# An expert's gathered tokens in three tiles instead of two, and the sums of hT inside the branch

## The chip, the core and the metric

The kernel runs on one core of a Trainium2 chip. The metric is the device time of one execution in microseconds (us). Three timed runs of the kernel before gave 5443.06, 5445.47 and 5447.21 us; the median is 5445.47 us. A profiled execution of the same kernel is what the prediction reads.

TensorE multiplies, VectorE and ScalarE work on tiles in on-chip memory, GpSimd issues the indirect transfers (gathers and scatters by index), and SyncE's queue issues nearly all other transfers. The profile calls them PE (with PEld for its weight loads), DVE, ACT, POOL and SP.

## What is computed

One decoder layer in f32: `x` of 8 sequences x 512 tokens x 512 features goes through a Mamba block, a cross-attention with 16 heads, and a mixture of experts, each followed by a residual sum and a layer norm. Only the last part matters here; the reference cut to it:

```
cap = int(1.25 * N * K / E)            # N = 4096 tokens, K = 4, E = 32: cap = 640
w, idx = _gate(xf, wg)                 # 4 experts and 4 weights for each token
...                                    # place of each token in its experts' buffers
xe = xp[buf_tok].reshape(E, cap, DIM)
h = silu(einsum('ecd,edh->ech', xe, w1)) * einsum('ecd,edh->ech', xe, w3)
out = einsum('ech,ehd->ecd', h, w2) * buf_w.reshape(E, cap, 1)
y = zeros((N + 1, DIM)).at[buf_tok].add(out.reshape(E * cap, DIM))[:N]
z = silu(xf @ sw1) * (xf @ sw3) @ sw2  # a shared expert, for all tokens
return (y + z).reshape(shape)
```

All three matrices of an expert are 512 x 512. An expert has room for 640 tokens; how many it gets depends on the data.

## The kernel before

`program` runs three stages: `layers` (Mamba, attention, the gate, the shared expert, and a scatter of every token's row into `xbuf`, ordered by expert), `experts` (32 experts, one after the other), and `finish` (the last layer norm). The diff touches `experts` alone.

**What an expert does.** `load(e)` starts four transfers on SyncE's queue (ScalarE's for the weights of expert 0): the tile `xe` with the expert's 640 gathered rows, five groups j = 0 to 4 of 128 rows, each row with its 32 expert weights and its token number behind it, and the weights w1, w3 and w2. `flip` turns one group's rows by four PE transposes into PSUM (`ps_t`, two buffers), and DVE copies them into `xT`. The matmuls are done by a Strassen scheme: seven products of half-sized blocks instead of eight, at the price of sums on DVE: `sums_w` makes the four sums of w1 and of w3, `sums_x` those of xT, `sums_w2` those of w2, and `sums_w(got, "hT")` those of `hT`, the hidden layer. `hidden` computes hT = silu(x w1) * (x w3) in two halves r; `give` computes hT w2, multiplies by the tokens' weights (`use` on DVE, `keep` on ACT), and `put(j)` adds each group of 128 result rows into `based` by an indirect DMA that GpSimd issues. The adding transfers go one after the other.

**The branch.** `hidden` comes in four copies, for 224, 256, 288 or 320 columns in a half; `tc.Switch` jumps to the copy that the number of the expert's tokens asks for (`arm`, a table written by the gate). A copy also holds the first two flips of the next expert and `fifth`, the product of the last group of rows (at 288 and 320 columns; otherwise DVE clears that result). PE, ACT and DVE each jump into a copy and, at its end, out of it to the code that all copies share. Each of the three engines announces its next jump ahead of time: `announce` places a load of the table's entry and a prefetch hint behind a given instruction of that engine.

**The order.** All instructions are written in program order, unrolled over the 32 experts. A planner that works with its own cost model may reorder them within a block, but nothing moves across the edge of a copy. In iteration e, `load(e + 1)` comes first, then the branch with `hidden(e)`, the next expert's first two flips and `fifth(e)`, then `give(e)`. Into `give` the helper `between` mixes the next expert's remaining flips, its `sums_w` of w3 and its `sums_x`.

**Buffers.** `xe`, `xT` and the weights have two buffers each (`p2` and `wp` have `bufs=2`), `hT` and its sums one. The tile xe of expert e is in use until the last `put` of expert e has landed, since the token numbers in it steer that transfer. So `xe` of expert e + 2 goes into the buffer of expert e, and its transfer waits for that landing.

In the profile the lines are: `xe` transfer L1258, weight transfers L1261, transposes L1294, their copies L1296, sums of w1, w3 and hT L1288, sums of xT L1303 to L1306, sums of w2 L1321, all products L1328 (`ps_h` in `hidden`, `ps_o` in `give`), ACT's copies L1343 and L1415, DVE's work in `hidden` L1350 and L1354, DVE's clearing of unused columns at the head of a copy L1521, `fifth` L1398, DVE's additions in `use` L1421, and `put` L1424.

Of the kernel before, what the change touches and what calls it, by code (L numbers as in the profile page):

```python
# [8 lines left out]
F32 = mybir.dt.float32  # L9
# [3 lines left out]
ALU = mybir.AluOpType  # L13
# [4 lines left out]
P = 128  # L18
# [21 lines left out]
E = 32  # L40
# [7 lines left out]
CJ = CAP // P  # L48
# [3 lines left out]
ROW = D + E + 1  # L52
# [1175 lines left out]
def experts(ctx, tc, a, xbuf, based, arm):  # L1228
# [11 lines left out]
    nc = tc.nc  # L1240
    cp = ctx.enter_context(tc.tile_pool(name="e_const", bufs=1))
    wp = ctx.enter_context(tc.tile_pool(name="e_w", bufs=2))
    p2 = ctx.enter_context(tc.tile_pool(name="e_p2", bufs=2))
# [7 lines left out]
    FH = D // 2  # L1251

    def load(e):
        got = {}
        got["x"] = xe = p2.tile([P, CJ, ROW], F32, tag="xe", name="xe")

        start = nc.sync.dma_start if e else nc.scalar.dma_start
        nc.sync.dma_start(xe, xbuf[e * CAP : (e + 1) * CAP, :].rearrange("(j p) d -> p j d", p=P))  # L1258
        for n in ("w1", "w3", "w2"):
            got[n] = w = wp.tile([P, DC, D], F32, tag=n, name=n)  # L1260
            start(w, a[n][e].rearrange("(c p) f -> p c f", p=P))  # L1261
        return got

    def A(w, i, j):
        return w[:, 2 * j : 2 * j + 2, i * FH : (i + 1) * FH]

    def BW(w, j, k):
        return w[:, 2 * j : 2 * j + 2, k * FH : (k + 1) * FH]
# [4 lines left out]
    def room_w(got, n):  # L1273

        s1, s2, s4 = (wp.tile([P, 2, FH], F32, tag=f"{n}s{i}", name="s", bufs=1 if n == "hT" else 2) for i in (1, 2, 4))
        got[n, "s"] = s1, s2, A(got[n], 1, 0), s4

    def sums_w(got, n):

        w = got[n]  # L1280
        s1, s2, _, s4 = got[n, "s"]
        for o, x, y, op in (
            (s1, A(w, 1, 0), A(w, 1, 1), ALU.add),
            (s2, s1, A(w, 0, 0), ALU.subtract),
            (A(w, 1, 0), A(w, 0, 0), A(w, 1, 0), ALU.subtract),
            (s4, A(w, 0, 1), s2, ALU.subtract),
        ):
            yield nc.vector.tensor_tensor(o, x, y, op)  # L1288

    def flip(got, j):  # L1290

        ps = pst.tile([P, D], F32, tag="tr", name="ps_t")
        for dc in range(DC):
            nc.tensor.transpose(ps[:, dc * P : (dc + 1) * P], got["x"][:, j, dc * P : (dc + 1) * P], ident)  # L1294
        to = got["xT"].rearrange("p c (k t) -> p c k t", k=2)[:, :, :, j * P // 2 : (j + 1) * P // 2]
        nc.vector.tensor_copy(to, ps.rearrange("p (c t k) -> p c k t", c=DC, k=2))  # L1296
# [11 lines left out]
    def room_w2(got):  # L1308
        got["t2"] = [wp.tile([P, 2, FH], F32, tag=f"w2t{i}", name="t", bufs=1) for i in range(4)]

    def sums_w2(got):

        w = got["w2"]
        t1, t2, t3, t4 = got["t2"]
        for o, x, y in (
            (t1, BW(w, 0, 1), BW(w, 0, 0)),
            (t2, BW(w, 1, 1), t1),
            (t3, BW(w, 1, 1), BW(w, 0, 1)),
            (t4, BW(w, 1, 0), t2),
        ):  # L1320
            nc.vector.tensor_tensor(o, x, y, ALU.subtract)  # L1321
            yield

    def product(ps, w, r, x, more=False):

        cols = ps.shape[-1]
        for n in range(2):
            ins = nc.tensor.matmul(  # L1328
                ps, w[:, n, r * P : (r + 1) * P], x[:, n, 0:cols], start=not more and n == 0, stop=n == 1,
                skip_group_check=more,  # L1330
            )
        return ins
# [57 lines left out]
    def fifth(e, got, cols):  # L1390

        j, y = CJ - 1, got["y"][CJ - 1]
        if 2 * cols <= j * P:
            nc.vector.memset(y, 0.0)
            return
        po = pso.tile([P, D], F32, tag="po", name="po")
        for ic in range(DC):
            nc.tensor.matmul(  # L1398
                po, got["hT"][:, ic, j * P : (j + 1) * P], got["w2"][:, ic, :], start=(ic == 0), stop=(ic == DC - 1)
            )  # L1400
        nc.scalar.activation(y, po, AF.Identity, scale=got["x"][:, j, D + e : D + e + 1])

    def give(e, got, side, which):

        xe, hT, w2 = got["x"], got["hT"], got["w2"]
        t1, t2, t3, t4 = got["t2"]
        both = range(2)
        ys = got["y"]

        def weight(j):  # L1410
            return xe[:, j, D + e : D + e + 1]

        def keep(ps, r, tag, j):
            v = p2.tile([P, HALF], F32, tag=f"{tag}{r}", name=tag)[:, 0:FH]
            ins = nc.scalar.activation(v, ps, AF.Identity, scale=weight(j))  # L1415
            if tag == "p1" and r and e + 1 < E:
                announce(which, e + 1, ins)
            return v

        def use(j, k, ps, more):  # L1420
            nc.vector.scalar_tensor_tensor(ys[j][:, k * FH : (k + 1) * FH], ps, weight(j), more, ALU.mult, ALU.add)  # L1421

        def put(j):
            nc.gpsimd.indirect_dma_start(  # L1424
                out=based,
                out_offset=bass.IndirectOffsetOnAxis(ap=xe.bitcast(I32)[:, j, D + E :], axis=0),
                in_=ys[j],
                in_offset=None,
                bounds_check=N + P - 1,
                compute_op=ALU.add,  # L1430
            )

        room_w(got, "hT")
        for ins in sums_w(got, "hT"):
            pass
        if e + 1 < E:
            announce(which, e + 1, ins)
        s1, s2, s3, s4 = got["hT", "s"]
        next(side, None)
        xs, p1, pu, p5 = [], [], [], []  # L1440
        for r in both:
            xs.append(psx.tile([P, HALF], F32, tag="h", name="ps_o")[:, 0:FH])
            product(xs[r], A(hT, 0, 0), r, BW(w2, 0, 0))
            p1.append(keep(xs[r], r, "p1", r))

        put(CJ - 1)
        next(side, None)
        for r in both:
            ps = psy.tile([P, HALF], F32, tag="h2", name="ps_o")[:, 0:FH]
            ins = product(ps, A(hT, 0, 1), r, BW(w2, 1, 0))  # L1450
            use(r, 0, ps, p1[r])
        if e + 1 < E:
            announce(which, e + 1, ins)
        for r in both:
            product(xs[r], s2, r, t2, more=True)
            pu.append(keep(xs[r], r, "pu", r))
        next(side, None)
        zs = []
        for r in both:
            zs.append(psy.tile([P, HALF], F32, tag="h2", name="ps_o")[:, 0:FH])  # L1460
            product(zs[r], s1, r, t1)
            p5.append(keep(zs[r], r, "p5", 2 + r))
        for r in both:
            product(xs[r], s3, r, t3, more=True)
            use(2 + r, 1, xs[r], p5[r])
        next(side, None)
        for r in both:
            product(zs[r], s4, r, BW(w2, 1, 1), more=True)
            use(r, 1, zs[r], pu[r])
            put(r)  # L1470
        next(side, None)
        for r in both:
            product(xs[r], A(hT, 1, 1), r, t4, more=True)
            nc.scalar.activation(ys[2 + r][:, 0:FH], xs[r], AF.Identity, scale=weight(2 + r))
            put(2 + r)
# [16 lines left out]
    def choice(k, e):  # L1492
        return engines[k].value_load(arm[0:1, e : e + 1])

    def announce(which, e, ins):
        k = ins.ins.engine
        with tc.issue_after(ins.ins):
            which[k] = choice(k, e)
            tc.switch_hint({k: which[k]}, len(COLS), label=f"cols{e}")
# [10 lines left out]
    which = {k: choice(k, 0) for k in engines}  # L1510
    for e in range(E):
        got, nxt = nxt, load(e + 1) if e + 1 < E else None
        got["hT"] = p2.tile([P, DC, CAP], F32, tag="hT", name="hT", bufs=1)
        room_w2(got)
        got["y"] = [p2.tile([P, D], F32, tag="y", name="y", bufs=CJ + 2) for j in range(CJ)]
        if nxt:
            nxt["xT"] = p2.tile([P, DC, CAP], F32, tag="xT", name="xT")
            room_w(nxt, "w1")
        for n in tc.Switch(which, len(COLS), hint=f"cols{e}" if e else None):
            if COLS[n] < HALF:  # L1520
                nc.vector.memset(got["hT"][:, :, 2 * COLS[n] :], 0.0)  # L1521
            for r in range(2):
                side = sums_w2(got) if r == 0 else sums_w(nxt, "w1") if nxt else iter(())
                hidden(got, r, side, COLS[n])
            if nxt:
                for j in range(2):
                    flip(nxt, j)
            fifth(e, got, COLS[n])
        give(e, got, between(nxt) if nxt else iter(()), which)
# [95 lines left out]
```

## Time and profile before

| what | value |
|---|---|
| median of three runs | 5445.47 us (5443.06 to 5447.21) |
| the profiled execution's own time | 5449.73 us |
| its span, first to last instruction | 5448.0 us |
| granted clock of PE, mean | 0.925 |
| PE busy | 4531.9 us, 83% |
| DVE busy | 4204.0 us, 77% |
| ACT busy | 2549.7 us, 47% |
| first expert's first product, by the timeline | 3800.5 us |
| last expert's first product | 5338.1 us |
| copies taken by the 32 experts | 12 at 224 columns, 5 at 256, 6 at 288, 9 at 320 |

The span is from the first instruction to the last; the execution's own time has 1.7 us around it. Busy shares are means over stages: up to about 3780 us the `layers` stage runs, in which DVE is busiest; the expert stage takes the 1580 us after it, about 49 us for each expert. A line of the waits names the engine, the tile it writes and its line, then what it waited for, the sum of those waits, how many there were, and the longest. A row of the timeline has the start, the duration, the engine, the line, output <- input, shapes, a count, and in brackets the idle time before it with what ended it. "issue" is idle time in which the engine waited for nothing that the profile shows. The columns of the windows are the busy time of each engine, the granted clock of PE and the DMA engines' busy share. The count of copies is from the shapes of the products in `hidden`.

### The profile page before, as it was taken

The numbers are of one execution on the slowest core, as the hardware profiler recorded it, in microseconds if no ns is written. First come the engines' busy times: TensorE is split into PE (matmuls) and PEld (weight loads), VectorE is DVE, ScalarE is ACT, GpSimd is POOL, SyncE is SP. The second block draws the span as 40 slices with busy tenths as digits, with TensorE's granted clock in tenths as the row PEclk, the third lists the DMA queues.
The fourth block names the chain that finished last, engine by engine and source line by source line (L and its number), as shares of the span: only waits on it lengthen the run. The fifth ranks groups of instructions, "written<-read, shape, count | busy, mean of one in ns | idle before, by whom it ended". The sixth has DMA issues, their size and how long they took to land.

```text
span 5448.0 us, 55096 instructions
## 1 busy us (share of the span) xinstructions
PE 4531.9 (83%) x17184; PEld 2469.3 (45%) x17184; DVE 4204.0 (77%) x5412; ACT 2549.7 (47%) x5709; POOL 569.6 (10%) x426
## 2 busy tenths in 40 slices
PE   6768889888888888978888888788978789898984
PEld 3324334234333433423433343233777667767773
DVE  7999899989989889998898988833555555555554
ACT  5566565665655556556565565422222222222223
POOL 1000002002002000200200200001111111111111
PEclk7879989999999998999999999898999999999997
DMA  8875337355435534635543553342454444444445
GB/s 240 266 217 144 93 92 212 75 124 170 119 100 152 151 96 98 204 77 133 165 117 99 154 146 94 85 135 82 106 131 104 128 120 126 109 128 120 114 119 156
DMA packets 486691, 721.80 MB, mean 132 GB/s; under 512 B 117137, under 2 KB 200625, under 8 KB 484096
## 3 DMA queue, kind: packets, MB, share of 16 engines
q1 hardware_dynamic: 450128, 627.16, 40.5%
q0 software_dynamic: 33280, 76.90, 7.3%
q10 hardware_dynamic: 2736, 11.54, 0.5%
q8 instruction: 211, 3.46, 0.3%
q14 instruction: 336, 2.75, 0.1%
HBM read 391.24 MB, written 165.05 MB: 102 GB/s over the span
## 4 chain that ended last, share of the span: by engine, by line
DVE 37%; PE 23%; DMA 16%; issue 16%; ACT 6%; SPq 2%; DVEq 0%; POOL 0%; POOLq 0%; ACTq 0%
DVE h L502 14%; DMA based<-y,xe 9%; PE ps_h L1328 6%; DVE h L495 5%; DVE h L511 5%; PE ps_p L758 3%; PE po L553 3%; DVE mx L823 2%; DVE xs L378 2%; PE ps_s L821 2%; ACT l_da L481 2%; PE ps_t L847 2%; PE po L863 2%; PE ps_o L1328 1%; PE py L522 1%
## 5 line engine op out<-in xcount | busy, mean ns | idle before, releaser
L481 ACT ACTIVATE l_da<-rep,l_aneg 128x256 f32<-128x256 f32 x2048 | 893.7, 499 | 942.8 <-DVE h L502 877.7
L502 DVE TENSOR_TENSOR_SCAN h<-l_da,h 128x1028 f32<-128x1028 f32 x512 | 1163.6, 2286 | 20.9 <-ACT l_da L481 18.4
L495 DVE TENSOR_TENSOR h<-rep,bc 128x1024 f32<-128x1024 f32 x512 | 612.6, 1213 | 108.4 <-PE py L522 90.6
L511 DVE TENSOR_TENSOR h<-h,bc 128x1024 f32<-128x1024 f32 x512 | 617.1, 1212 | 2.1
L522 PE MATMUL py<-h,l_fold 128*32 128x512 f32 x2048 | 369.5, 647 | 110.9 <-DVE h L511 94.2
L821 PE MATMUL ps_s<-l_ka,l_qa 64*128 64x512 f32 x1024 | 328.8, 714 | 140.8 <-DVE mx L823 140.3
L1424 POOL DMA_INDIRECT based<-y,xe x160 | 254.6, 1591 | 1355.9 <-DVE y L1421 530.0
L1328 PE MATMUL ps_h<-xT,w 128*128 128x224 f32 (+3 forms) x1536 | 375.2, 395 | 14.2 <-issue 10.4
L823 DVE TENSOR_REDUCE mx<-ps_s 128x2 f32<-128x1024 f32 x256 | 309.6, 1214 | 61.2 <-PE ps_s L821 60.7
L863 PE MATMUL po<-eT,l_va 128*64 128x512 f32 x1024 | 303.1, 673 | 47.1 <-ACT eT L851 42.1
L1328 PEld LDWEIGHTS ps_h<-xT,w 128*128 128x128 f32 x1536 | 296.3, 193 | 71.9 <-issue 13.1
L847 PE MATMUL ps_t<-l_qa,l_ka 64*128 64x512 f32 x1024 | 304.6, 666 | 24.1 <-ACT eT L851 23.3
L851 ACT ACTIVATE eT<-ps_t 128x1024 f32<-128x1024 f32 x256 | 258.8, 1015 | 128.2 <-PE ps_t L847 128.1
L696 POOL DMA_INDIRECT xbuf<-x2t,dest x128 | 217.2, 1697 | 863.8 <-DVE dest L680 764.2
L1328 PE MATMUL ps_h<-t,s 128*128 128x224 f32 (+3 forms) x1024 | 253.1, 396 | 34.5 <-DVE hT L1350 21.0
L344 PE MATMUL ps_z<-xnT,wm 128*128 128x256 f32 x1024 | 238.8, 390 | 29.6 <-DVE o L562 24.2
L553 PE MATMUL po<-wm,zs 128*128 128x512 f32 x512 | 246.6, 637 | 13.4 <-DVE z L965 11.7
L758 PE MATMUL ps_p<-x2T,wa 128*128 128x512 f32 x512 | 242.3, 628 | 18.0 <-ACT hT L952 10.4
L1350 DVE TENSOR_TENSOR hT<-ps_h,p 128x224 f32<-128x224 f32 (+3 forms) x128 | 55.8, 436 | 260.5 <-PE ps_h L1328 259.5
L344 PE MATMUL ps_x<-xnT,wm 128*128 128x256 f32 x1024 | 247.6, 394 | 4.5 <-ACT xnT L333 2.5
L344 PEld LDWEIGHTS ps_z<-xnT,wm 128*128 128x128 f32 x1024 | 195.6, 194 | 92.0 <-DVE o L562 37.4
L344 PEld LDWEIGHTS ps_x<-xnT,wm 128*128 128x128 f32 x1024 | 196.9, 196 | 82.2 <-issue 45.1
(237 smaller groups left out, 7011.1 us busy)
## 6 DMA issues: line engine op xcount, KB each, us to landing
w<-in_w SPq DMA_DIRECT2D x93, 1024.0 KB
wm<-in_in_proj_w SPq DMA_DIRECT2D x128, 512.0 KB
rep<-dt SPq DMA_DIRECT2D x256, 256.0 KB
rep<-dtx SPq DMA_DIRECT2D x256, 256.0 KB
xbuf<-zero SPq DMA_DIRECT2D x32, 1362.5 KB
xe<-xbuf SPq DMA_DIRECT2D x32, 1362.5 KB
wm<-in_out_proj_w SPq DMA_DIRECT2D x64, 512.0 KB
wa<-in_sw SPq DMA_DIRECT2D x24, 1024.0 KB
```

Source lines behind the costliest of these rows:

```text
L344: nc.tensor.matmul(ps[:, i, :], w[:, dc, i * P : (i + 1) * P], f["xnT"][:, dc, :], start=(dc == 0), stop=(dc == DC - 1),)
L481: nc.scalar.activation(da[:, n, 1:], dt[:, j, i, :], AF.Exp, scale=aneg[:, 2 * q + i, 2 * jj + j, g : g + 1])
L495: nc.vector.tensor_tensor(h[:, :, 1:], dtx.rearrange("p j i t -> p (j i) t"), f["bc", g][0], ALU.mult)
L502: nc.vector.tensor_tensor_scan(flat, da.rearrange("p n t -> p (n t)"), flat, 0.0, ALU.mult, ALU.add)
L511: nc.vector.tensor_tensor(h[:, :, 0:T], h[:, :, 1:], f["bc", g][1], ALU.mult)
L522: nc.tensor.matmul(f["py"][j * QP : (j + 1) * QP, :, :], fold, hs[j // 2][:, 2 * (j % 2) : 2 * (j % 2) + 2, 0:T], start=False, stop=g == N ...
L553: nc.tensor.matmul(pos[j], yg[:, c, j * P : (j + 1) * P], w[:, i, :], start=(c == 0), stop=(c == CC - 1))
L821: nc.tensor.matmul(ps[:, j, :], qa[r, lt * P : (lt + 1) * P], ka[r, :], start=True, stop=True)
L823: return lambda: nc.vector.tensor_reduce(mx[:, lt, :].unsqueeze(2), ps, AX.X, ALU.max) and None
L847: nc.tensor.matmul(ps[:, j, :], ka[r, kc * P : (kc + 1) * P], qa[r, :], start=True, stop=True)
L863: nc.tensor.matmul(po[j * 2 * HD : (j + 1) * 2 * HD, :], va[:, kc, i, j * HD : (j + 2) * HD], eT[:, j, :], start=(kc == 0), stop=(kc == SC ...
L1328: ins = nc.tensor.matmul(ps, w[:, n, r * P : (r + 1) * P], x[:, n, 0:cols], start=not more and n == 0, stop=n == 1, skip_group_check=more,)
```

## The change

Three things:

- `xe` gets a third buffer. Expert e + 3 now shares a buffer with expert e.
- The four sums of hT on DVE move from the start of `give` into each of the four copies, behind `hidden` and ahead of the two flips. Their tiles are taken before the branch.
- DVE's announcement of the next jump had stood behind the last of those sums. It now stands behind the second of the first two additions (`use(r, 0, ...)`) in `give`, beside PE's announcement. For that `use` returns its instruction.

```
@@ load
-        got["x"] = xe = p2.tile([P, CJ, ROW], F32, tag="xe", name="xe")
+        got["x"] = xe = p2.tile([P, CJ, ROW], F32, tag="xe", name="xe", bufs=3)
@@ give
         def use(j, k, ps, more):
-            nc.vector.scalar_tensor_tensor(ys[j][:, k * FH : (k + 1) * FH], ps, weight(j), more, ALU.mult, ALU.add)
+            return nc.vector.scalar_tensor_tensor(
+                ys[j][:, k * FH : (k + 1) * FH], ps, weight(j), more, ALU.mult, ALU.add
+            )
...
-        room_w(got, "hT")
-        for ins in sums_w(got, "hT"):
-            pass
-        if e + 1 < E:
-            announce(which, e + 1, ins)
         s1, s2, s3, s4 = got["hT", "s"]
...
         for r in both:
             ps = psy.tile([P, HALF], F32, tag="h2", name="ps_o")[:, 0:FH]
             ins = product(ps, A(hT, 0, 1), r, BW(w2, 1, 0))
-            use(r, 0, ps, p1[r])
+            out = use(r, 0, ps, p1[r])
         if e + 1 < E:
             announce(which, e + 1, ins)
+            announce(which, e + 1, out)
@@ the loop over experts
         room_w2(got)
+        room_w(got, "hT")
...
                 hidden(got, r, side, COLS[n])
+            for _ in sums_w(got, "hT"):
+                pass
             if nxt:
                 for j in range(2):
                     flip(nxt, j)
```

More of the change, by code (lines that the diff above doesn't have):

```diff
@@ L1254, in load @@
         got = {}
-        got["x"] = xe = p2.tile([P, CJ, ROW], F32, tag="xe", name="xe")
+        got["x"] = xe = p2.tile([P, CJ, ROW], F32, tag="xe", name="xe", bufs=3)
         start = nc.sync.dma_start if e else nc.scalar.dma_start
@@ L1420, in use @@
         def use(j, k, ps, more):
-            nc.vector.scalar_tensor_tensor(ys[j][:, k * FH : (k + 1) * FH], ps, weight(j), more, ALU.mult, ALU.add)
+            return nc.vector.scalar_tensor_tensor(
+                ys[j][:, k * FH : (k + 1) * FH], ps, weight(j), more, ALU.mult, ALU.add
+            )
         def put(j):
@@ L1431, in put @@
             )
[L1433 to L1437, printed above, removed]
         s1, s2, s3, s4 = got["hT", "s"]
@@ L1450, in give @@
             ins = product(ps, A(hT, 0, 1), r, BW(w2, 1, 0))
-            use(r, 0, ps, p1[r])
+            out = use(r, 0, ps, p1[r])
         if e + 1 < E:
             announce(which, e + 1, ins)
+            announce(which, e + 1, out)
         for r in both:
@@ L1514, in experts @@
         room_w2(got)
+        room_w(got, "hT")
         got["y"] = [p2.tile([P, D], F32, tag="y", name="y", bufs=CJ + 2) for j in range(CJ)]
@@ L1524, in experts @@
                 hidden(got, r, side, COLS[n])
+            for _ in sums_w(got, "hT"):
+                pass
             if nxt:
```

## The prediction

> **What bounds the kernel now.** I read the waits of the expert stage first, then the timeline of single experts. The waits, in total, number and longest:
>
> ```profile
> DVE s L1288 <- issue: 107.5, 23, 6.1
> ...
> PE ps_t L1294 <- DMA xe<-xbuf: 81.9, 16, 10.5
> ...
> PE ps_o L1328 <- DVE s L1288: 27.0, 16, 3.6
> ...
> PE ps_h L1328 <- DVE hT L1350: 21.0, 24, 2.6
> ```
>
> The second line is the one that the third tile aims at: TensorE waits for xe 81.9 us (10.5 of it ahead of the first expert, which no tile can help; 71.4 inside the stage). The first and third belong to the sums of hT. Where xe's wait comes from shows in the chain of waits and on SyncE's queue, in expert 10 (224 columns):
>
> ```profile
> 4315.47 4.77 DMA based<-y,xe
> ```
>
> ```profile
> 4320.43 0.37 SPq L1258 DMA_DIRECT2D xe<-xbuf  x1
> ```
>
> The last put of expert 9 lands at 4320.24; the transfer of expert 11's xe starts at 4320.43, as both share a buffer. TensorE in the same stretch:
>
> ```profile
> 4317.51 1.68 PE L1328 MATMUL ps_h<-t,w 128*128 128x224 f32 x8
> 4328.10 3.05 PE L1294 MATMUL ps_t<-e_ident,xe 128*128 128x128 f32 x12 [8.90 <-DMA xe<-xbuf]
> ...
> 4347.69 1.49 PE L1328 MATMUL ps_h<-xT,w 128*128 128x224 f32 x7
> ```
>
> TensorE ends `hidden` at 4319.2, idles 8.90 us until xe has landed, and starts the next expert at 4347.69. I call the time from the end of `hidden` to the next expert's first product the tail: here 28.5 us. The loop is xe, flips, products, four puts that go one after the other, next xe; it takes 48 to 53 us in nearly every expert, whatever its columns. Only where `hidden` is short (22.05 us at 224 columns against 31 to 34 at 320) does TensorE come to the flips before xe.
>
> Expert 14, also of 224 columns, found its xe landed, and so shows what the stage is like without that wait. TensorE, then VectorE:
>
> ```profile
> 4525.74 0.63 PE L1294 MATMUL ps_t<-e_ident,xe 128*128 128x128 f32 x4 [0.44 <-DVE xT L1296]
> ...
> 4532.94 3.50 PE L1328 MATMUL ps_o<-t,s 128*128 128x256 f32 x8 [2.68 <-DVE s L1288]
> ...
> 4542.63 1.99 PE L1328 MATMUL ps_o<-t,hT 128*128 128x256 f32 x8 [0.42 <-DVE y L1421]
> ```
>
> ```profile
> 4524.90 1.29 DVE L1296 COPY xT<-ps_t 128x512 f32<-128x512 f32 x2
> 4531.38 0.69 DVE L1288 TENSOR_TENSOR s<-hT 128x512 f32<-128x512 f32 x1 [5.19 <-issue]
> ...
> 4533.92 1.28 DVE L1296 COPY xT<-ps_t 128x512 f32<-128x512 f32 x2
> ...
> 4542.10 0.87 DVE L1421 SCALAR_TENSOR_TENSOR y<-ps_o,xe,p 128x256 f32<-128x256 f32 x2
> ```
>
> Tail: 4524.4 to 4544.4, 20.0 us. VectorE copies the two flips, leaves the copy by a jump and idles 5.19 us on "issue", and only then makes the sums of hT, for which TensorE waits 2.68 us. From 4531.38 VectorE works without a gap to its last additions, and TensorE waits 0.42 us for the first two of those: VectorE's line of work sets this tail. At 320 columns (the last copy, left without a jump) no such idle time shows, and the tail is TensorE's, 18.4 to 19.2 us in seven of nine.
>
> **The third tile.** It removes the wait for the landing in all experts: the transfer of expert e+2 then needs the puts of e-1, which land about 21 us into `hidden(e)`, and its flips come over 40 us later. The transfer is moved on SyncE's queue ahead of w1, w3 and w2 of its own expert. If it stands there for the puts (landed 21 to 23 us into an expert), w1 and w3 behind it, which need the end of `hidden(e)` (22 us at the earliest), lose at most about 1 us; by the DMA queue they land 9 us after issue, and VectorE's first sum of w1 comes 23 us after it. No other queue is passed. A tile takes 640/128 x 545 x 4 = 10.9 KB of a partition and no time.
>
> The gain, by tails read off the timeline. Nine experts at 224 columns waited 3.9 to 8.9 us: 26.8, 27.1, 27.7, 23.6, 27.4, 28.5, 26.4, 28.3, 26.9 us, together 242.7. For the new tail I take 20.3: the two experts of that kind without the wait have 20.0 (14) and 20.9 (29), and 256 columns 21.0. 9 x 20.3 = 182.7, a gain of 60.0. Expert 30 loses its 5.85 us. Three experts with 0.9 to 1.4 us of wait (6, 19, 22) go from 22.4, 21.1, 22.5 to 20.3, 19.9, 20.3: 5.5. Sum 71.4.
>
> **The clock.** After xe's waits TensorE runs at half clock for a while. Windows of it (stretch, its length, busy time and count of PE, PEld, DVE, ACT and POOL, then the granted clock, third from the right):
>
> ```profile
> 4321.60:4331.80 10.20, 3.68 (x15) 3.15 (x16) 1.38 (x2) 0.00 (x0) 1.01 (x1) 0.50 0.99 325
> 4533.20:4536.60 3.40, 3.40 (x10) 2.59 (x10) 3.40 (x7) 0.59 (x2) 0.00 (x0) 0.50 0.02 5
> 4132.00:4142.00 10.00, 5.69 (x27) 4.61 (x28) 8.09 (x14) 1.90 (x4) 0.00 (x0) 1.00 0.16 51
> ```
>
> The first row follows the 8.90 us wait; the second follows expert 14's 2.68 us for the sums; ahead of the third's middle TensorE waited 3.44 us and kept full clock. Of six waits of 2.7 to 3.6 us for the sums, two were followed by half clock. The Trainium skill (TensorE: Matmul & The Clock Gate, What's actually happening) says that an idle window of about 3.4 us halves the clock; by it the shorter waits that this change leaves would cost nothing. The rows allow up to 3.4 us at half clock, 1.7 us of work, after a third of them. I count none, since VectorE sets those tails, and keep 17 x 1.7 / 3 = 10 us for the range.
>
> **The sums of hT.** Per expert four instructions (0.69, 0.69, 0.68, 0.68 us, starting 0.6 apart: 2.5 us) move on VectorE ahead of two copies (1.3 us) and of the jump. In expert 14, from the end of `hidden`: sums 0.5 to 3.0, copies 3.0 to 4.3, idle 5.2, next copies at 9.5. Before: copies 0.5 to 1.8, idle 5.2, sums 7.0 to 9.5, next copies at 9.5. The line has the same pieces in another order, so its end stays. What waits for the moved sums now is the pair of copies: the third flip needs a PSUM buffer that the first copy empties, at 3.7 instead of 1.2, so TensorE idles about 2.4 us there in the 17 experts that have no `fifth` to cover it (its products take 3.6 us in the timeline, at 288 and 320). It then reaches its s2 product at about 8.2, finds the sums ready (instead of 2.68 us of waiting) and is held by VectorE's first additions at about 12.0 instead of 12.4. So of the 27.0 us of waits for the sums I credit 3: 0.7 in each of experts 9, 13 and 29, where the first copies had to wait for TensorE, and 1.2 in the last, where nothing follows, as VectorE's next wait takes the rest.
>
> Against that, the idle time of the jump out. It was 4.5 to 6.1 us where the jump fell into the weight transfers that start as `hidden` ends, 3.9 to 4.7 where xe had delayed it past them, and 2.2 and 2.5 for the last two experts, which load nothing. The jump now comes 2.5 us later, deeper into those transfers: I allow 0.3 us, which is in the 20.3, and at 288 columns a tail of 19.9 where four of six have 19.5 to 19.7: a loss of 1. Net: a gain of 2.
>
> **The announcement.** The load and the hint go from behind the sums (8.5 us or more ahead of the jump) to behind the second addition (about 5 us). Queued behind them on VectorE are the last two sums of w3; the load takes 0.3 us of its sequencer, under a 0.68 us sum. Jumps to the 224 copy, the first in order, show 1.1 to 1.4 us of idle time before L1521 in eleven of twelve cases; jumps to the 256 and 288 copies 2.6 to 4.3 us in ten of eleven, though announced. If the later hint made those prompt, TensorE would get back at most the 21.0 us that it waits for L1350, less 0.3 in each 224 expert: 17. If it made the 224 jumps late too, the one such case (into expert 5, TensorE waiting 2.63 instead of 0.29) prices it: 11 x 2.3 = 26 lost. I take nothing: jumps announced 8 to 14 us ahead came equally late, so the lead is not what decides. The Trainium skill (Runtime: NRT & Kernel Launch, Instruction fetch mechanics) speaks against this change: an engine but TensorE holds two fetch blocks, and a taken branch out of them waits for a transfer. By it no hint's place helps VectorE, the jumps stay, and the sum is the same.
>
> **Sum.** 71.4 + 2 = 73 us. From the profiled 5449.7 that gives 5376.4; that execution lay 4.3 us above the median, so I predict 5372.
>
> **Rivals.** *Eaten by VectorE (19%).* With xe gone, VectorE's jump of 5 to 6 us and its sums are late next, everywhere, and the delayed copies cost what I hid: 1.5 us in 23 experts is 35, leaving a gain of 20 to 50, 5395 to 5425. For it: the tail is VectorE's already. Against: expert 14 shows that tail, and I used it. *More than I count (10%).* The hint works and half of the 24 us of waits for the sums that I did not credit go too: 73 + 17 + 12 = 102, 5343. Against: the line of VectorE has no shorter order. *The transfer is not early (3%).* The planner leaves xe behind a wait on SyncE's queue and the time stays within 0.2%. Against: even behind w2 it starts as `give` ends, 22 us ahead of its flips. *Slower (6%).* The third flip's 2.4 us of idling comes out on the path, with the clock halved after each: 2.4 + 3.4 = 5.8 us in the 17 experts up to 256 columns is 99, minus 73: 26 slower, 5471. It decides from 73 / 17 = 4.3 us for each of them. For it: half clock after 2.68 us. Against: six such waits gave it twice.
>
> **How the numbers follow.** The forecast, a gain of 55 to 95, has 62%. 0.2% is 11 us, about what a measurement of this kernel can tell from no change. The range goes down by the hint's 17 and 15 of the waits for the sums (5340) and up by the jumps' 35 (5407); what lies outside is the rivals' far ends. Faster 0.91, same 0.03, slower 0.06.
>
> **What would show it.** Right: no wait for xe but the first 10.5 us, no row of sums behind "issue" (the idle time now stands before a copy, L1296, still about 5 us in 23 experts), TensorE's waits for the sums at zero, new ones of 2 to 3 us before L1294, tails near 20 us in all experts, and a mean clock above 0.925. Wrong: waits for xe that stay; tails of 22 and more; or heads of the 256 to 320 copies without idle time, which would put the hint to work.

## The result and the profile after

The changed kernel takes 5494.43 us (median of four runs, 5482.32 to 5503.45) against 5445.4 us in the same session: a ratio of 1.0084, 95% interval 1.0071 to 1.0096. By the ratio it is slower by about 46 us (49 by the medians), where 73 less was predicted. The profiled execution took 5503.45 us, its span is 5501.7 us, the granted clock 0.917. Of the 53.7 us by which the spans differ, 9.7 lie ahead of the first expert's first product (3810.2 us against 3800.5); in the profiles of the experiments, none of which touches that stage, this point lies anywhere from 3789 to 3807, so I put no cause to it. The expert stage, from the first product to the last, is 44.7 us longer: 1621.9 us against 1577.2. What follows it is 0.7 us shorter.

The waits of the expert stage after, in the form shown of before:

```profile
PE ps_o L1328 <- DVE y L1421: 141.8, 31, 11.2
DVE s L1288 <- DMA w<-in_w: 114.7, 24, 10.3
...
ACT p L1343 <- issue: 78.8, 15, 5.7
...
PE ps_h L1328 <- ACT p L1343: 37.2, 19, 3.1
...
PE ps_t L1294 <- DVE xT L1296: 22.5, 23, 1.6
...
PE ps_t L1294 <- DMA xe<-xbuf: 10.8, 1, 10.8
```

The same rows of the kernel before, where the prediction does not show them:

```profile
PE ps_o L1328 <- DVE y L1421: 28.2, 35, 0.9
...
ACT p L1343 <- issue: 20.2, 4, 5.4
...
PE ps_h L1328 <- ACT p L1343: 13.3, 10, 2.8
...
DVE s L1288 <- DMA w<-in_w: 9.7, 7, 1.8
```

The third tile did what it says: TensorE waits for xe ahead of the first expert and nowhere else (81.9 us before). The sums of hT are no longer waited for (27.0 before), and their row behind "issue" is gone. In their place TensorE waits 141.8 us for VectorE's first additions (28.2 before), and VectorE 114.7 us for a weight (9.7 before). Those two are one thing. Expert 14 again, which the prediction had taken as its model, VectorE first:

```profile
4556.46 0.69 DVE L1296 COPY xT<-ps_t 128x512 f32<-128x512 f32 x1 [4.29 <-PE ps_o L1328]
4562.86 0.69 DVE L1288 TENSOR_TENSOR s<-w 128x512 f32<-128x512 f32 x1 [5.71 <-DMA w<-in_w]
4563.58 0.69 DVE L1288 TENSOR_TENSOR s<-s,w 128x512 f32<-128x512 f32 x1
4564.19 0.68 DVE L1288 TENSOR_TENSOR w<-w 128x512 f32<-128x512 f32 x1
4564.79 0.68 DVE L1296 COPY xT<-ps_t 128x512 f32<-128x512 f32 x1
4565.40 0.68 DVE L1288 TENSOR_TENSOR s<-w,s 128x512 f32<-128x512 f32 x1
4565.99 0.87 DVE L1421 SCALAR_TENSOR_TENSOR y<-ps_o,xe,p 128x256 f32<-128x256 f32 x2
```

then TensorE, SyncE's queue, and the chain of waits:

```profile
4554.51 1.89 PE L1328 MATMUL ps_o<-t,s 128*128 128x256 f32 x8
4557.21 0.66 PE L1294 MATMUL ps_t<-e_ident,xe 128*128 128x128 f32 x4 [0.81 <-DVE xT L1296]
4566.53 3.78 PE L1328 MATMUL ps_o<-t,s 128*128 128x256 f32 x8 [8.67 <-DVE y L1421]
```

```profile
4548.19 0.37 SPq L1258 DMA_DIRECT2D xe<-xbuf  x1
4548.65 26.56 SPq L1261 DMA_DIRECT2D w<-in_w  x3
```

```profile
4549.22 13.61 DMA w<-in_w
...
4562.86 0.70 DVE s L1288
```

TensorE ends `hidden` at 4547.95; xe's transfer starts at 4548.19 and w1's and w3's at once behind it. VectorE idles 4.29 us behind the jump (the profile puts this wait down to a product, but the flip that the copy reads had ended 5.9 us before). It copies the third flip, and then, before the fourth flip and the first additions, stands 5.71 us for w3, until 4562.86. It makes three sums of w3, a copy, the fourth sum, and only then the additions, at 4565.99, 18.1 us after `hidden`. TensorE has idled 8.67 us for them, and its next products run at half clock: eight of one kind take 3.78 us where eight of the same kind took 1.89 before the wait, and the windows (columns as in the prediction) give

```profile
4550.00:4557.50 7.50, 6.65 (x35) 5.36 (x36) 2.86 (x5) 1.89 (x4) 0.58 (x1) 1.00 1.01 298
4566.50:4573.00 6.50, 6.47 (x17) 5.23 (x18) 4.57 (x7) 0.95 (x2) 0.00 (x0) 0.55 0.00 0
4573.00:4580.00 7.00, 7.00 (x31) 5.56 (x30) 2.00 (x4) 0.95 (x2) 1.54 (x1) 1.00 0.53 157
```

The tail is 28.4 us; in the profile before this expert had 20.0.

Why VectorE waits there shows in the compiled order of its instructions behind the jump out of a copy (s3 a sum of w3, sh a sum of hT, c2 to c4 the copies of the later flips, x the four sums of xT, y the additions, A the announcement):

```
before   jump  sh sh sh sh A c2 c3 s3 y s3 y s3 s3 c4 x y y y y
after    jump  c2 s3 s3 s3 c3 s3 y y A c4 x y y y y
```

In both kernels the w3 that is summed in the tail of expert e is that of expert e + 2, although `between` writes these sums into the code one expert later. The count of the rows shows it: the tail of expert 30 has no sum of w3, while each tail before it has four. The planner takes them ahead across a whole branch, which my account of the order ("nothing moves across the edge of a copy") left out. That w3 goes into the buffer that `hidden(e)` has just left, so it is still in transfer in this very tail.

### The profile page after: what moved, and what is told of

Read it like the earlier page. It is cut to its first block, busy times and chain, and to the rows that moved or that the text cites. A ratio compares the mean times of both kernels' runs of the same rounds, so it can differ in the third digit from the quotient of the medians.

```text
span 5501.7 us, 55062 instructions
## 1 busy us (share of the span) xinstructions
PE 4553.3 (83%) x17184; PEld 2485.9 (45%) x17184; DVE 4212.8 (77%) x5412; ACT 2547.1 (46%) x5709; POOL 571.0 (10%) x426
## 4 chain that ended last, share of the span: by engine, by line
DVE 37%; PE 33%; issue 11%; DMA 10%; ACT 6%; SPq 2%; DVEq 0%; POOL 0%; ACTq 0%; POOLq 0%
DVE h L502 15%; PE ps_h L1328 12%; PE ps_o L1328 5%; DVE h L495 5%; DVE h L511 5%; PE ps_p L758 4%; DMA w<-in_w 4%; DVE xs L378 2%; DVE mx L823 2%; PE po L553 2%; PE ps_s L821 2%; DMA based<-y,xe 2%; ACT l_da L481 2%; PE po L863 2%; PE ps_t L847 2%
## 5 line engine op out<-in xcount | busy, mean ns | idle before, releaser
L1328 PE MATMUL ps_h<-t,s 128*128 128x224 f32 (+3 forms) x1024 | 261.6, 407 | 45.2 <-ACT p L1343 37.2
L1328 PE MATMUL ps_o<-t,s 128*128 128x256 f32 x512 | 154.9, 456 | 147.4 <-DVE y L1421 141.8
L344 PE MATMUL ps_z<-xnT,wm 128*128 128x256 f32 x1024 | 239.6, 390 | 30.0 <-DVE o L562 24.2
L1328 PEld LDWEIGHTS ps_h<-t,s 128*128 128x128 f32 x1024 | 197.2, 197 | 102.3 <-ACT p L1343 46.1
```

The lines of the kernel that those rows point to most:

```text
L344: nc.tensor.matmul(ps[:, i, :], w[:, dc, i * P : (i + 1) * P], f["xnT"][:, dc, :], start=(dc == 0), stop=(dc == DC - 1),)
L1328: ins = nc.tensor.matmul(ps, w[:, n, r * P : (r + 1) * P], x[:, n, 0:cols], start=not more and n == 0, stop=n == 1, skip_group_check=more,)
```

## The experiments

Two theories, mainly. A: the loss is this order, in which sums of a w3 still in transfer stand ahead of the first additions. B: the sums inside the copies or the late announcement cost by themselves. The first expectations name a third, C: the third tile itself costs, by its transfers. The results together; "tail" is the mean tail of the twelve 224-column experts, "addition" their mean time from the end of `hidden` to the first addition, "hidden" and "stage" sums over all experts, all from the profiled executions. Each session timed the kernel before again (medians 5445 to 5456 us), so the ratios are what compares.

| kernel | median us | ratio to before, 95% | stage | hidden | tail | addition |
|---|---|---|---|---|---|---|
| before | 5445.4 | 1 | 1577.2 | 870.3 | 25.5 | 16.8 |
| changed | 5494.4 | 1.0084 [1.0071, 1.0096] | 1621.9 | 885.2 | 27.1 | 17.5 |
| e1 third tile only | 5406.7 | 0.9922 [0.9900, 0.9945] | 1537.7 | 870.2 | 23.6 | 14.2 |
| e2 without third tile | 5478.0 | 1.0057 [1.0040, 1.0074] | 1613.1 | 881.0 | 26.3 | 18.4 |
| e3 additions first | 5376.0 | 0.9862 [0.9839, 0.9884] | 1498.3 | 852.5 | 22.5 | 9.4 |
| e4 own w3, additions first | 5325.4 | 0.9771 [0.9751, 0.9792] | 1463.9 | 860.0 | 18.9 | 9.5 |
| e5 changed, xe behind w3 | 5437.0 | 0.9957 [0.9942, 0.9972] | 1554.6 | 881.3 | 21.6 | 12.2 |
| e6 announcement only | 5461.7 | 1.0009 [0.9996, 1.0021] | 1586.6 | 876.4 | 25.4 | 16.8 |
| e7 e4, sums of hT in give | 5363.2 | 0.9820 [0.9803, 0.9837] | 1493.5 | 867.4 | 19.7 | 9.8 |
| e8 e4, w2 early | 5311.4 | 0.9720 [0.9702, 0.9738] | 1439.7 | 835.8 | 18.9 | 9.6 |
| e9 e4, two tiles | 5416.2 | 0.9938 [0.9920, 0.9957] | 1535.1 | 860.2 | 24.3 | 14.9 |
| e10 changed, w2 early | 5421.6 | 0.9937 [0.9916, 0.9957] | 1553.9 | 849.9 | 24.3 | 14.8 |
| e11 e8, xe last | 5311.6 | 0.9742 [0.9725, 0.9760] | 1445.1 | 838.2 | 19.2 | 9.9 |
| e12 third tile, xe behind w3 | 5362.5 | 0.9843 [0.9822, 0.9863] | 1493.8 | 867.9 | 19.8 | 11.1 |

**e1: the third tile alone.** The kernel before with `bufs=3` on xe.

> The kernel before with three tiles for xe, and nothing else of the change. Theory A (the loss is VectorE's order: the sums of a w3 that is still in transfer stand ahead of the first additions, and TensorE waits for those): VectorE's order is that of before, C C s(w3) y, so the 71 us of waits for xe go, but the first sum of w3 now meets the end of the transfer, about 14.5 to 16.5 us after the last product of hidden in an expert of 224 columns, and the first addition follows 0.7 us later instead of at 16.8 on average: 1 to 2 us in each of eleven such experts and 6 in expert 30, so 5420 to 5435 us, TensorE's waits for y over 60 us. Theory B (the sums inside the copies and the late announcement are what costs): the prediction's 71 us are seen here, 5370 to 5385. Theory C (the third tile itself costs, by its transfers): 5450 or more.

Between A's range and B's, 13 us from the one and 22 from the other: a gain of 0.78%, some 43 us. C, which had no gain, falls. The waits are A's:

```profile
PE ps_o L1328 <- DVE y L1421: 61.0, 31, 9.5
...
DVE s L1288 <- DMA w<-in_w: 54.5, 19, 8.8
```

The wait for xe is gone and a smaller one has come in its place, at the next transfer in the queue. With VectorE's old order (c2 c3 s3 y) the first addition is behind one sum of w3, and it comes 14.2 us after `hidden` instead of 16.8.

**e2: the other two parts alone.** The changed kernel with `bufs=2` on xe.

> The changed kernel with two tiles for xe: the sums of hT in the copies and the moved announcement alone. VectorE's order after the jump is that of the changed kernel, C s(w3) s(w3) s(w3) C s(w3) y y. Theory A: the loss is here too: the waits for xe are back (some 70 to 80 us), but w3 lands at the same time, so the first additions come no later than with three tiles; in the experts of 320 columns they come at 12 us after hidden as in the changed kernel (10 before); 5480 to 5505 us. Theory B: 5494 plus the 71 us of the tile, 5550 to 5570. Theory C: 5440 to 5450.

5478 us, 0.57% slower, some 31 us; A's range missed by 2 us, B's by 72, C's by 28. VectorE's order in the trace is that of the changed kernel, so the loss is there without the third tile. The third tile on top of it gains nothing: the first additions come 1.0 us sooner (17.5 against 18.4), the tails at 224 columns are 0.9 us longer.

**e3 and e4: the order mended.** e3 has one edge more than the changed kernel:

```
-            next(sums, None)
+            if j == 2 and outs:               # outs: the second of each expert's two first additions
+                with tc.issue_after(outs[-1].ins):
+                    next(sums, None)
+            else:
+                next(sums, None)
```

in `between`, where `outs[-1]` is the addition of the expert before, so the w3 of expert e + 2 is still summed in expert e, but behind the additions. e4 starts the sums only at `j == CJ - 1`, behind the addition of the expert in whose code they are written, so that they cannot be taken ahead: expert e then sums the w3 of expert e + 1, which landed an expert ago (the tail of expert 30 now has its four sums). Both give VectorE the same order, `jump c2 c3 y y A s3 s3 s3 c4 s3 x y y y y`; they differ in whose w3 it is.

> The changed kernel with one edge more: the first sum of the next-but-one expert's w3 is issued after this expert's first additions. VectorE's order becomes C C y y s(w3) s(w3) s(w3) C s(w3), then the sums of xT. Theory A: the first additions come 6 to 10 us after hidden at 224 columns (17.5 in the changed kernel), TensorE's 142 us of waits for them fall under 40; but VectorE still stands for w3 before the copy of j=4 and the sums of xT, so tails at 224 columns are 24 to 25 us (27.1), at 320 columns 19 (21.1): 5425 to 5460 us. Theory B: 5480 to 5500.

> The changed kernel with the sums of w3 held behind the first additions of the expert they belong to, so that none is done one expert ahead: same order on VectorE as in the run above, but the w3 that is summed landed an expert ago. Theory A: no wait for w3 is left (114.7 us in the changed kernel), tails at 224 columns 17 to 19 us, at 320 columns 18.5 to 19.5: 5360 to 5390 us. Theory B: 5480 to 5500.

Both are faster than before. e3 is 49 us below its range and e4 35 us below, 2.3% under before and about 3% under the changed kernel. In expert 14 of e4:

```profile
4452.24 1.29 DVE L1296 COPY xT<-ps_t 128x512 f32<-128x512 f32 x2 [4.07 <-PE ps_o L1328]
4453.44 0.87 DVE L1421 SCALAR_TENSOR_TENSOR y<-ps_o,xe,p 128x256 f32<-128x256 f32 x2
4454.23 0.68 DVE L1288 TENSOR_TENSOR s<-w 128x512 f32<-128x512 f32 x1
```

```profile
4453.97 1.99 PE L1328 MATMUL ps_o<-t,s 128*128 128x256 f32 x8 [0.33 <-DVE y L1421]
```

The first additions start 9.5 us after `hidden`, TensorE waits 0.33 us for them, and the tail is 18.8 us. No row of VectorE waiting for a weight is left in the stage. e3 keeps 31.9 us of it, now ahead of c4 and the sums of xT, and its tails are 3.6 us longer. That is the price of the transfer with the same order. Not all of the gain is in the tails: `hidden` is 32.7 us shorter in e3 and 25.2 in e4 than in the changed kernel, and there w2 is issued earlier too (see e8 and e10). B predicted no change for both and falls.

**e5: the transfer made earlier, the order left bad.** xe's DMA is moved in `load`.

> The changed kernel with the DMA of xe issued behind that of w3 on SyncE's queue, where it stands ahead of w1 now; VectorE's order is untouched. Theory A (the first additions wait for the landing of w3): in experts of 224 columns w1 no longer waits on the queue for the last put of the expert before, and w3 lands some 5 us earlier, before xe's 1.36 MB: first additions at 12 to 13 us after hidden (17.45), 12 experts by 4.5, about 50 us off: 5435 to 5455 us, VectorE's 114.7 us of waits for w under 60. Rival (the additions are late for the jump or for the sums in the copies): nothing, 5480 to 5500.

```
-        nc.sync.dma_start(xe, ...)            # ahead of the loop over w1, w3, w2
...
+            if n == "w3":                     # ins: w3's DMA
+                with tc.issue_after(ins.ins) if e else ExitStack():
+                    nc.sync.dma_start(xe, ...)
```

The time is in the range. The ratio falls by 0.0127 from that of the changed kernel, about 69 us, more than the 50 expected; the first additions come at 12.2 us, the expected place. The waits (lines are two further down in this kernel):

```profile
PE ps_o L1330 <- DVE y L1423: 72.1, 31, 5.4
...
DVE s L1290 <- DMA w<-in_w: 40.0, 16, 4.4
```

In the changed kernel w1 is issued 23.7 us into a 224-column expert on average, 0.5 us behind xe, which waits for the last put of the expert before; here at 21.3, with xe at 24.3. So both things that A names, the order and the landing, each move the additions by themselves.

**e6: the announcement alone.** The kernel before, `use` returning its instruction, with

```
         for ins in sums_w(got, "hT"):
             pass
-        if e + 1 < E:
-            announce(which, e + 1, ins)
...
             announce(which, e + 1, ins)
+            announce(which, e + 1, out)
```

> The kernel before with VectorE's jump announced behind its second first addition, 6 us later than there, and nothing else. Prediction's step: nothing, 5435 to 5457 us, the idle time before the next expert's first VectorE work (25.7 us in 8 experts) unchanged. Rival (the late announcement makes VectorE miss its jump in the experts that are announced in time now): 1 to 3 us in 20 experts, 5465 to 5500.

1.0009, interval 0.9996 to 1.0021: no difference that can be measured. (The median lies 5 us above the range, in a session whose kernel before lay 11 us above that of the first.)

**e7: what the sums inside the copies are worth.** e4 with the sums of hT and the announcement back in `give`.

> The kernel before with three tiles for xe and the sums of w3 held behind the first additions of their own expert; the sums of hT and the announcement stay behind the jump. It shows what the sums inside the copies are worth once no w3 is waited for. Theory A: VectorE jumps 2 us earlier and then has 2.8 us of sums ahead of the copies, so the first additions come about 1 us later than in the run with all of the change (9.5 at 224 columns), 23 experts by 1: 5335 to 5355 us. The prediction's step (2 us in all): 5320 to 5335.

0.9820 against 0.9771, about 27 us between them, where I had estimated 23; the median is 8 us above the range, and the prediction's 2 us fall. The announcement moved together with the sums here, so the 27 us belong to both. By the profiles 22.6 us are in the tails and 7.4 in `hidden`. Tails at 256 columns are 2.6 us longer than in e4 (mean of four, one of them by 6.8), at 224 0.8.

**e9: what the third tile is worth with the order mended.** e4 with `bufs=2` on xe.

> The kernel of e4 with two tiles for xe, as before. It shows what the third tile is worth once VectorE's order is right. Prediction's step (71 us of waits for xe, all on the path): e4's time and 70 to 90 us, 5395 to 5415 us, tails at 224 columns of 25 to 26 us instead of 18.9. Rival (some of the wait for xe lies beside VectorE's idle time around its jump, as in the kernel of before): 30 to 45 us, 5355 to 5370.

0.9938 against 0.9771: some 91 us by the medians' ratios, 71 by the stages of the two profiles. The wait for xe is back, and this time most of it shows in the tails: 24.3 against 18.9 us, 65 us in twelve experts. The smaller rival falls.

**e12: the prediction's model made true.** The kernel before with the third tile, and xe's DMA behind w3's as in e5.

> The kernel before with three tiles for xe and xe's DMA behind w3's on SyncE's queue; VectorE's order, the sums of hT and the announcement as before. It makes in every expert what expert 14 of the profile before had by chance: xe landed, and w1 and w3 alone on the queue after hidden. Theory A (the prediction's model tail of 20.3 us left out that xe's transfer then ran ahead of w3's): VectorE no longer waits for w3 (54.5 us in e1), tails at 224 columns 20 to 21 us (23.6 in e1): 12 by 3, some 35 to 40 us below e1, 5365 to 5380 us, where the prediction had put the third tile. Rival (in e1 something else holds the tails): 5395 to 5412.

5362.5 us, 1.57% under before and slightly below the range: tails of 19.8 us, where the prediction had put 20.3. VectorE waits 13.6 us for weights instead of 54.5, and its order is that of e1, so the place of xe's transfer in the queue makes the difference.

**e8, e10, e11: the copies' heads.** I call the time from TensorE's first product of an expert to ScalarE's first copy the head. The changed kernel also lost 14.9 us in `hidden`. TensorE waits there for ScalarE's first copies (37.2 us after, 13.3 before), which come late behind its jump into a copy (the row of "issue" at L1343 went from 20.2 to 78.8 us). In the copies for 256 columns and more, across the profiles, this head goes with the time at which w2's 1 MB transfer is issued: in the kernel before, nine heads with w2 issued 2.6 us ahead of the first product are 3.5 to 3.9 us long, and six with 1.5 to 1.8 us are 4.6 to 6.1; in the changed kernel it is issued 1.5 us ahead in 17 of the 18 such cases, and those heads are 4.8 to 6.4. (The tile that the new w2 goes into is last read by the last group of products but one in `give`; before, TensorE then waited up to 0.9 us for additions ahead of the last group, which it no longer does, having waited earlier.) Theory D is that this transfer, being under way, makes the code that the jump goes to arrive late. e8 is e4, e10 the changed kernel, both with

```
-            got[n] = w = wp.tile([P, DC, D], F32, tag=n, name=n)
-            start(w, a[n][e].rearrange("(c p) f -> p c f", p=P))
+            got[n] = w = wp.tile([P, DC, D], F32, tag=n, name=n, bufs=3 if n == "w2" else 2)
+            with tc.issue_after(ins.ins) if e and n == "w2" else ExitStack():   # behind w3's
+                ins = start(w, a[n][e].rearrange("(c p) f -> p c f", p=P))
```

> The kernel of e4 with three tiles for w2 and w2's DMA issued right behind w3's, so that its 1 MB is not under way when ScalarE jumps into the next expert's copy. Theory D (ScalarE's missed jump takes longer while w2 is transferred: first copy of p1 at 3.5 us where w2 was issued 2.6 us before the first product, 5.9 where 1.5, 2.4 where 7): heads of 2.2 to 2.6 us instead of 3.8 in the 20 experts of 256 columns and more, 20 by 1.4: 5290 to 5305 us. Rival (the later heads are those of a jump announced or waited for otherwise): heads as in e4, 5318 to 5332.

> The changed kernel with three tiles for w2 and w2's DMA right behind w3's, VectorE's order untouched. It shows how much of the loss is the transfer of w2 at the jump. Theory D: ScalarE's first copies in the 20 experts of 256 columns and more at 3.1 to 3.4 us (5.4 to 5.6 in the changed kernel), hidden there shorter by 1.5 to 2 us: 30 to 40 us off, 5450 to 5465 us. Rival (the late heads come from the announcement): 5485 to 5500.

In e10 `hidden` shrinks by 35.3 us in all, as D has it. The heads go from 5.7 to 4.0 us on average, not to the 3.1 to 3.4 that I wrote, and what holds the rest was not tried. TensorE's wait for ScalarE's copies falls from 37.2 us (the line is one further down):

```profile
PE ps_h L1329 <- ACT p L1344: 8.4, 14, 1.3
```

The whole gain is larger than I expected, 0.0147 in the ratio or 80 us (the median is 28 us below the range), since the tails fall too, by 32.8 us in all. w2's transfer no longer runs beside the first put: in the first three of the 224-column experts the second put, which waits for the first, starts 3.8 to 4.1 us into the expert instead of 6.4 to 8.4. Over all of them xe is issued 3.3 us earlier, and w1 and w3 some 2.3. In e8 the gain is 28 us, as expected in sum (the median is 6 us above the range), 24.2 of it in `hidden`. ScalarE's 18 heads fall only from 3.9 to 3.3 us on average, not to 2.4, so more than half of the 24.2 us must lie elsewhere; VectorE's own jump is a candidate (its wait behind "issue" at L1321, one line further down in e8, goes from 25.3 to 12.3 us). How it divides was not tried.

> The kernel of e8 with xe's DMA behind w2's, so that SyncE's queue for a load is w1, w3, w2, xe and no weight waits for the last put of an expert. Since no work in the tail waits for a weight in e8 any more, theory A expects no gain that can be measured: 5300 to 5315 us. Rival (the weights' later start still delays the jumps' code): 5280 to 5300.

No gain, as A has it: 5311.6 us against e8's 5311.4 in another session (0.9742 against 0.9720, intervals that overlap). With e11, e8 is the fastest kernel of the study, 2.8% under before [0.9702, 0.9738].

## Why the prediction was wrong

**The tail of 20.3 us** is the step that failed first. It was read off experts 14 and 29, the two that had not waited for xe, and taken for "what the stage is like without that wait". They had something else besides. Before each of them an expert had run long (53.7 and 57.0 us), so xe's transfer started while `hidden` still ran. SyncE's queue in the kernel before, around expert 14 and in expert 10:

```profile
4516.74 0.37 SPq L1258 DMA_DIRECT2D xe<-xbuf  x1
4523.70 18.91 SPq L1261 DMA_DIRECT2D w<-in_w  x3
```

```profile
4321.07 24.39 SPq L1261 DMA_DIRECT2D w<-in_w  x3
```

(These are the weights issued in expert 10's tail; its xe was issued at 4320.43, as the prediction shows.) In expert 14 the weights start 7.0 us behind xe, when its packets are through (they start from 4517.8 to 4522.6). In eight of the nine 224-column experts that wait for xe they start 0.6 us behind it, as in expert 10. The packets of xe run ahead of those of w1 and w3 (in the changed kernel's expert 11 xe's from 4397 to 4402, the weights' from 4401 to 4409), and where VectorE stands waiting for w3 it has it 14 to 16.5 us after `hidden` in the changed kernel, and 11.5 to 16.5 in e1. In the kernel before that was hidden: VectorE, late by the wait for xe, came to its first sum of w3 after 14 to 19 us and found it landed. So the wait for xe covered most of the wait for w3, and with the third tile alone 43 of the 71 us came, at tails of 23.6 us instead of 20.3. Expert 14 itself goes from 20.0 to 24.8 us in e1. e12 gives every expert what expert 14 had and gets the predicted size and more (some 85 us, tails of 19.8); e9 against e4 has the 71 us of waits on the path, too. The term was sized right for a queue that the kernel does not have. The prediction looked at this queue, but held the landing against VectorE's first sum of w1, 23 us later, and not against that of w3, which comes in the same tail.

**"The same pieces in another order, so its end stays"** is the step that turned the sign. I reordered the pieces by hand and left the rest of VectorE's line as it was. The planner did not: with the sums of hT gone from behind the jump it put all sums of w3 ahead of the first additions. e2 prices the second and third part of the change at a loss of 31 us together, where a gain of 2 stood, and on top of the third tile they cost 1.6% (e1 against the changed kernel), since TensorE now waits in one piece of up to 11.2 us. e3, the changed kernel with that order mended, is 1.4% under before. Why the planner's costs came out so was not tried.

**The credit of 2 us for the sums** had the right sign only where no weight is waited for, and there less than a tenth of the size: 27 us (e7 against e4). It had let VectorE's next wait take all but 3 us of what the moved sums free; which of the later steps gave the rest was not tried.

**The announcement at nothing** was right in the kernel before (e6); in the mended order it was tried only together with the sums. **The clock at nothing** was not: over the stage it went from 0.965 to 0.944 in the profile after, and to 0.994 in e4's, where TensorE's waits are short; its busy time in the stage, for the same products, went from 1387.9 us to 1399.6 and to 1361.2. The Trainium skill (TensorE: Matmul & The Clock Gate, What's actually happening) has the clock halve after about 3.4 us without work; the 0.55 behind the wait of 8.67 us agrees, and so do the full-clock rows around it. The half clock behind a wait of only 2.68 us, which the prediction shows, does not, and there the measurement decides.

**The heads** were taken as unchanged. The 14.9 us in `hidden` go with w2's transfer beside the jump: e10, which moves it, gets back 35.3.

**The rivals.** The slower one was right in sign alone. Its third flip does wait (22.5 us in 23 cases, 1.6 at most, where 2.4 each was written), with no half clock behind it in expert 14 (the first row of the windows). "Eaten by VectorE" had the right engine with the wrong work. That w1 and w3 would lose at most about 1 us by xe on the queue was about right on average (they are issued 0.7 us later), but what mattered was xe's own transfer ahead of them, some 5 us, which was there before as well.

Of the signs listed, the waits for xe and the sums came as written, and the idle time ahead of a copy nearly so (18 experts, 4.2 us each, booked as a wait for a product). The clock, 0.917, fell where a rise above 0.925 was listed, and tails of 27 us instead of 20 are what it said would prove it wrong.

## What to carry to other kernels

When a wait is to be removed, look up what lands next behind the thing waited for, in the same queue: a case that happened to run without the wait may also have had that next transfer early. Where a planner orders an engine's work, moving one block can move others past it, so read the compiled order behind the move, and tie work that needs a fresh transfer behind the work that another engine waits for. Here such an edge alone turned a loss of 0.8% into a gain of 1.4%, and 2.3% where the sums also took a weight that had long landed.

## What the runs showed of the hardware

I had not expected a jump to depend so much on other transfers. Over eleven profiles, ScalarE's first copy in the 256- to 320-column copies comes 5.6 us after TensorE's first product (mean of 87) where w2's 1 MB is issued 1 to 1.8 us ahead of that product, 3.8 (35) where 2.4 to 3, and 3.3 (7) where 5 or more. The trace's packets of the kind "instruction" show where the time goes. In the profiles before and after, ScalarE's first copy starts in each of 36 cases (18 in either) 1.6 to 2.0 us behind an 8 KB packet of that kind. This packet starts 1.7 to 2.0 us after the first product in the nine short heads of before, 2.7 to 4.4 in the six long ones, and 3.1 to 4.7 in the 17 of after, where w2's own packets run mostly from 0.5 us ahead of that product to 4 us behind it. Which engine's code a packet holds, the trace does not say. The Trainium skill (Runtime: NRT & Kernel Launch, Instruction fetch mechanics) says that a jump out of the fetched pages needs a DMA transfer before the engine goes on; the rows agree with that, and add that with a large transfer started just before, the packet and the copy come up to some 2 us later. Moving the transfer away shortened the heads by 1.7 us in e10 and 0.6 in e8.
